# Null-key attention folded into differences, and the key transposes moved to another PSUM bank

## The chip, the cores and the metric

The kernel runs on one core of a Trainium2 chip. The metric is device time in microseconds (us) from one launch. Three runs of the kernel before gave 1120.65, 1121.5 and 1123.69 us; the median is 1121.5 us. For this kernel a difference under about 0.3% (3.4 us) cannot be told from no change.

The core has five engines with queues of their own. In the profile PE is the matrix engine (PEld its weight loads), DVE the vector engine, ACT the scalar engine, POOL the general-purpose engine and SP a queue that only issues transfers (DMAs). An engine works through its queue in order; a semaphore holds an instruction back until another engine or a transfer has done its part. SBUF is the core's working memory of 128 partitions; PSUM holds what PE writes, in banks.

## What is computed

`x` holds 64 sequences of 128 tokens with 512 channels. Attention has 16 heads of 64, and all heads share one set of keys and values. One more key and value, the null key and null value (`cond_64[0]` and `cond_64[1]`), stand in front of the 128 of each sequence, with a bias of their own per head, and the causal mask and the key mask spare them.

```
xn   = layernorm(x) * g_in
q    = (xn @ Wq) as 16 heads of 64, scaled by 1/8
k, v = xn @ Wkv                          # 64 columns each, shared by the heads
k    = [null_kv[0]; k]    v = [null_kv[1]; v]
sim  = q k^T + [null_bias | attn_bias]   # 129 columns
sim  = -max where key > token, or where the key is masked
out  = softmax(sim) v  ->  @ Wo  ->  layernorm * g_out
y    = x + out
```

A softmax is unchanged when the same number is taken from a whole row. Values can have a constant taken off and put back behind the softmax, since its weights sum to one.

## The kernel before

Sequences are blocks, numbered 0 to 63, and four make a group. One loop, `step(n)` for n from -6 to 62, interleaves the stages of different blocks by hand: in step n the values of block n are multiplied by the softmax, the scores of block n+2 are made, block n+1 goes through the exponentials, the keys and values of block n+6 are projected, and the queries of group (n+6)//4 are made. The order of the calls in `step` is the order of each engine's queue; nothing is reordered later. `part` is (n+6) mod 4, so it runs 0, 1, 2, 3, and even steps have part 0 or 2.

**PE.** Queries are made two blocks against two blocks with seven products in place of eight (`product`, line 422, banks "a", "c" and a "w"), the output projection likewise for pairs of blocks (`out_product`, line 750, banks "X", "Y" and a "w"). Pairs are blocks (1,2), (3,4) and so on up to (57,58). For a pair, products 1 and 2 and two `out_part` belong to the even step n = p+1, products 5, 6, 7 and 3 to the odd step n = p+2, and the layer norm and the residual to the even step n = p+3. So an odd step opens bank "Y" with product 5 (`pyY`), and an even step puts normalised outputs there (`yn`, line 804), one block after the other.

**The null key before.** The dot product of the queries with the null key is a linear function of the tokens, so 16 columns of weights (`wq` times the null key, summed per head, lines 862 to 880) are appended to the 128 columns of `wkv`. `kv_mm` (line 308) multiplies a block's tokens by these 144 columns, eight passes of PE per block. `kv_out` copies the keys (twice, side by side) to SBUF (line 320), and adds `vnb` to the 64 values and the 16 null scores (line 324). `nulls_move` brings values and null scores to the other half of the partitions with two copies on ACT (lines 332, 333) and two transfers on SP (lines 334, 337), in steps of part 3 and part 0. `null_copy` (line 475) puts the null scores into the first and the last column of the score tile `S`, which has 1+64+128+1 columns per head pair; `bias_add` (line 466) has filled the 192 between with bias plus mask.

**Bank "w" and the keys.** `ps_w` has two banks that are handed round. In each step `values` takes two for the attention output `po` (line 636), ACT empties them at the end of `values_end` (line 680), and the tile `pk` for the transposed keys (line 342) and for the key and value projection (line 308) takes the next. `pk` is made behind the query product 6, and read by DVE at the end of the step (lines 347, 320, 324).

**DVE in an even step.** From the instruction `done` (line 668), which waits for PE's first half of the attention output, the queue goes: residual of the second block of a pair (`pair_residual`, lines 808 and 809: `yn` times `gob` in place in bank "Y", then plus `res` into SBUF), the 32x32 transposes of the softmax (575), row maxima (513), the second scores (508), queries (443), row maxima (513), `kT` (347), `ktok` (320), `vs` (324).

**POOL in an even step** scales the softmax (line 543). In steps of part 0 it makes the four token differences `xS` for the next group as well (`token_sum`, line 404): one behind the first scale, and two behind the second. `out_sums` (730 to 733) follows.

**SP** issues the transfers; 14 of them move each block's transposed softmax (`aTb`, line 601).

Of the kernel before, what the change touches and what calls it, by code (L numbers as in the profile page):

```python
# [17 lines left out]
def kernel(  # L18
# [70 lines left out]
    KVN = 2 * DH + H  # L89
# [60 lines left out]
    nkb = const.tile([P, DH], FP, name="nkb")  # L150
    nvb = const.tile([P, DH], FP, name="nvb")
    nv2 = const.tile([P, 1], FP, name="nv2")
    nbh = const.tile([P, H], FP, name="nbh")
    biasp = const.tile([P, R8, NL + N], FP, name="biasp")
# [13 lines left out]
    for kc in (3, 1):  # L168
        nc.sync.dma_start(out=wq[:, kc, :], in_=wq_r[:, kc, :])
    nc.sync.dma_start(out=nkb, in_=cond[0].partition_broadcast(P))  # L170
    nc.sync.dma_start(
        out=wkv[:, :, 0 : 2 * DH], in_=w_kv.rearrange("(kc p) f -> p kc f", p=P)
    )

    def load_second():
        for m in (4, 5, 6):
            load_x(m)
        load_bias(1)
        load_mask(0)
        nc.sync.dma_start(out=nbh, in_=null_bias.partition_broadcast(P))  # L180
        nc.sync.dma_start(out=nvb, in_=cond[1].partition_broadcast(P))
        for r in range(2):
            nc.sync.dma_start(
                out=nv2[r * DH : (r + 1) * DH, :], in_=cond[1].unsqueeze(1)
            )

    def load_bias(u):
        rows = slice(u * DH, (u + 1) * DH)
        bias_r = attn_bias.rearrange("(u f r) i j -> u r i f j", u=2, r=2)[u]
        for r in range(2):  # L190
            rf = slice(r * NF, (r + 1) * NF)
            nc.sync.dma_start(out=biasp[rows, rf, 0:NL], in_=bias_r[r, 0:DH, :, 0:NL])
            nc.sync.dma_start(out=biasp[rows, rf, NL:], in_=bias_r[r, DH:N])

    def causal(u):

        rows = slice(0, P if u else DH)
        for keys, base in ((slice(0, NL), -DH * u), (slice(NL, NL + N), DH - DH * u)):
# [9 lines left out]

    def load_late():
# [7 lines left out]
    nc.gpsimd.memset(biasp[0:DH], 0.0)  # L217

# [7 lines left out]
    vnb = const.tile([P, DH + H], FP, name="vnb")  # L226
# [7 lines left out]
    xT, qT, kT, vs, nv, mneg = {}, {}, {}, {}, {}, {}  # L234
# [66 lines left out]
    ktok = {}  # L301

# [13 lines left out]

    def kv_out(m, pkv):
        g, t = divmod(m, GB)
        k = bp.tile([P, 2, DH], FP, tag="ktok", name=f"ktok_{m}")
        nc.vector.tensor_copy(k, pkv[:, 0:DH].unsqueeze(1).broadcast_to([P, 2, DH]))  # L320
        ktok[m] = k
        if t == 0:
            vs[g] = hp.tile([P, GB, DH + H], FP, tag="vs", name=f"vs_{g}", bufs=3)
        nc.vector.tensor_tensor(vs[g][:, t, :], pkv[:, DH:], vnb, ALU.add)

    def nulls_move(g, ts):

        if ts.start == 0:
            nv[g] = hp.tile([P, GB, DH + H], FP, tag="nv", name=f"nv_{g}")
        lo, hi = slice(0, DH), slice(DH, P)  # L330
        n1, n0 = slice(DH, DH + R8), slice(DH + R8, DH + H)
        nc.scalar.copy(nv[g][lo, ts, n1], vs[g][lo, ts, n0])
        nc.scalar.copy(nv[g][hi, ts, n0], vs[g][hi, ts, n1])
        nc.sync.dma_start(
            out=nv[g][hi, ts, 0 : DH + R8], in_=vs[g][lo, ts, 0 : DH + R8]
        )
        nc.sync.dma_start(out=nv[g][lo, ts, n0], in_=vs[g][hi, ts, n0])
# [110 lines left out]
    def mask_neg(g):  # L448
        mneg[g] = gp.tile([P, GB, NL + N], FP, tag="mneg", name=f"mneg_{g}", bufs=1)
        m8 = m8s.pop(g).rearrange("p (t j) -> p t j", t=GB)  # L450
        for keys, m in ((slice(0, NL), m8[:, :, 0:NL]), (slice(NL, NL + N), m8)):
            nc.vector.tensor_scalar(
                mneg[g][:, :, keys], m, 0.0, NEG, ALU.is_equal, ALU.mult
# [6 lines left out]
    def bias_add(b):  # L460
# [3 lines left out]
        else:  # L464
            S[b] = sp.tile([P, R8, ROW], FP, tag="s", name=f"s_{b}")
        nc.gpsimd.tensor_tensor(  # L466
            S[b][:, :, 1 : ROW - 1],
            biasp,
            mneg[g][:, t].unsqueeze(1).broadcast_to([P, R8, NL + N]),
            ALU.add,  # L470
        )

    def null_copy(b):
        g, t = divmod(b, GB)
        nc.gpsimd.tensor_copy(
            S[b][:, :, 0 : ROW : ROW - 1],
            nv[g][:, t, DH:].rearrange("p (k e) -> p e k", k=2),
        )

# [154 lines left out]
    def value_mm(b, u, half, keys, vals, slots, start=True):  # L634
        for r in range(2):
            nc.tensor.matmul(  # L636
                pos[b][u][r * DH : (r + 1) * DH, half],
                vals[keys, b % GB, 0:DH],
# [8 lines left out]
    def values(b, split):  # L647
# [6 lines left out]
        g = b // GB  # L654
# [5 lines left out]
        value_mm(b, 0, 0, lo, vs[g], slice(0, 2))  # L660
        value_mm(b, 1, 0, hi, nv[g], slice(0, 2))
        if split:
            value_mm(b, 0, 1, lo, vs[g], slice(2, 4))
            value_mm(b, 1, 1, hi, vs[g], slice(4, 6))
# [4 lines left out]
        else:  # L669
            value_mm(b, 0, 1, slice(0, P), vs[g], slice(2, 4))  # L670
            value_mm(b, 1, 1, slice(0, P), vs[g], slice(4, 6))

    def values_end(b, split):
        g = b // GB
        if split:
            value_mm(b, 1, 1, lo, vs[g], slice(4, 6), start=False)
            value_mm(b, 0, 1, hi, vs[g], slice(2, 4), start=False)
# [128 lines left out]
    def pair_residual(b):  # L806
        z = yn.pop(b)
        nc.vector.tensor_tensor(z, z, gob, ALU.mult)
        nc.vector.tensor_tensor(ys[b], z, res.pop(b), ALU.add)
# [42 lines left out]
    prods = {}  # L852

    def null_order(out, heads):

        for u in range(2):
            nc.vector.tensor_copy(
                out[:, (1 - u) * R8 : (2 - u) * R8].rearrange("p (r f) -> p r f", r=2),
                heads[:, u * R8 : (u + 1) * R8].rearrange("p (f r) -> p r f", r=2),
            )  # L860

    def weights_kv_prod(kc):

        pool, tag = ((sp, "s"), (sp, "s"), (hp, "sb"), (hp, "xb"))[kc]
        bufs = None if kc < 2 else 1
        prods[kc] = pool.tile([P, H, DH], FP, tag=tag, name=f"prod_{kc}", bufs=bufs)
        nc.gpsimd.tensor_tensor(
            prods[kc],
            wq[:, kc, :].rearrange("p (h d) -> p h d", d=DH),
            nkb.unsqueeze(1).broadcast_to([P, H, DH]),  # L870
            ALU.mult,
        )

    def weights_kv(kc):
        nc.vector.tensor_scalar(
# [438 lines left out]
```

## Time and profile before

| what | number |
|---|---|
| runs of the kernel, device time | 1120.65, 1121.5, 1123.69 us |
| profiled execution, first to last instruction | 1117.9 us |
| median of the runs less this span | 3.6 us |
| granted PE clock | 0.9 or more of full speed in all 40 slices |
| DMA engines | 116 GB/s mean, 2 to 6 tenths busy |
| `kv_mm` | 488 passes in the loop, 24 in the fill, 144 columns each |
| `null_copy` on POOL | 64 x 205 ns |

For the profiled execution its span is given and no other time; the three runs lie 2.8 to 5.8 us above that span. The page of the profile gives for each engine the busy time, its share of the span and the instructions; then the engines by slices of the span; the chain of work that ended last; and groups of instructions with their mean duration and the engine's idle time in front of them. Other views of the same trace give groups by shape, single stretches of time instruction by instruction, and the waits by who waited for whom. A row of a stretch reads: start in us, duration in us, engine, line, operation, output<-inputs, shape, count, and in brackets the idle time before it with what ended it.

### The profile page before, as it was taken

The page shows a single profiled execution, that of the slowest core. Times are in us where ns is not written, and L with a number is a line of the kernel's source. Part 1 is how long each engine was busy: PE and PEld are TensorE (multiplying, and loading weights), DVE is VectorE, ACT ScalarE, POOL GpSimd, SP SyncE. Part 2 cuts the span into 40 slices and gives each one's busy share as a digit, 9 for nine tenths or more (in the row PEclk, how much of TensorE's full clock was granted, in tenths as well). Part 3 has the DMA queues.
Part 4 walks back from the last instruction along what each step waited for, and adds up shares of the span by engine and source line. Part 5 has one row for each costly group of instructions (what it writes and reads, how often), then busy time and mean ns, then how long its engine had stood idle before and what let it go on. Part 6 is the DMA issues. An engine that isn't in the chain of part 4 may idle for free.

```text
span 1117.9 us, 27535 instructions
## 1 busy us (share of the span) xinstructions
PE 1088.6 (97%) x9794; PEld 875.1 (78%) x9794; DVE 808.8 (72%) x1743; ACT 676.5 (61%) x2709; POOL 743.0 (66%) x587
## 2 busy tenths in 40 slices
PE   8899999999999999999999999999999999999987
PEld 6576788888888788888888888888888888888633
DVE  6576578777768767777877877877776786666862
ACT  2365577565667566667656667756666765657651
POOL 6446967577676667758566676757767675677832
PEclk9999999999999999999999999999999999999999
DMA  5323244443634534354343534444353453422333
GB/s 189 125 70 71 79 137 125 128 118 91 169 97 126 132 108 131 101 149 113 128 127 89 159 100 138 124 128 119 93 168 99 125 133 114 106 68 76 98 106 99
DMA packets 107864, 130.09 MB, mean 116 GB/s; under 512 B 29264, under 2 KB 72528, under 8 KB 105936
## 3 DMA queue, kind: packets, MB, share of 16 engines
q1 hardware_dynamic: 106480, 126.96, 40.1%
q8 instruction: 78, 1.28, 0.5%
q10 hardware_dynamic: 1248, 1.38, 0.4%
q14 instruction: 58, 0.48, 0.1%
HBM read 54.86 MB, written 31.46 MB: 77 GB/s over the span
## 4 chain that ended last, share of the span: by engine, by line
PE 70%; DVE 7%; DMA 7%; SPq 6%; POOL 4%; issue 3%; ACT 3%; POOLq 0%; DVEq 0%; ACTq 0%
PE pa L422 15%; PE pyX L750 14%; PE pyY L750 7%; PE ps L495 7%; PE po L636 7%; PE pc L422 7%; DMA x<-in_x_dram 6%; SPq L601 4%; PE pk L308 4%; PE pw L422 3%; PE pyw L750 3%; PE py L697 2%; ACT s L522 2%; POOL s L466 1%; SPq L295 1%
## 5 line engine op out<-in xcount | busy, mean ns | idle before, releaser
L522 ACT ACTIVATE s<-s,nmax 128x65 f32<-128x65 f32 (+1 forms) x1024 | 372.0, 368 | 0.4
L466 POOL TENSOR_TENSOR s<-biasp,mneg 128x1536 f32<-128x1536 f32 x64 | 221.1, 3455 | 101.4 <-DVE sb L575 98.2
L543 POOL TENSOR_TENSOR s<-s,rinv 128x512 f32<-128x512 f32 (+1 forms) x128 | 189.3, 1479 | 122.8 <-DVE nmro L794 89.8
L680 ACT ACTIVATE oT<-po,nv 128x512 f32<-128x512 f32 x128 | 80.9, 683 | 200.1 <-PE po L636 198.8
L522 ACT ACTIVATION_READ_ACCUMULATOR s<-s,nmax 128x1 f32 x1024 | 194.7, 190 | 0.0
L750 PE MATMUL pyX<-wT,oT 128*128 128x256 f32 x696 | 164.8, 380 | 0.5 <-DVE kyu L762 0.5
L750 PEld LDWEIGHTS pyX<-wT,oT 128*128 128x128 f32 x696 | 131.8, 190 | 19.7 <-DVE kyu L762 0.9
L495 PEld LDWEIGHTS ps<-kT,qT 64*64 64x64 f32 x4096 | 94.2, 133 | 45.4 <-DVE s L508 23.1
L508 DVE TENSOR_TENSOR s<-ps,s 128x512 f32<-128x512 f32 (+1 forms) x128 | 121.5, 949 | 8.1 <-PE ps L495 6.6
L422 PE MATMUL pa<-xS,wq 128*128 128x256 f32 x480 | 123.5, 380 | 1.0 <-ACT ku L433 1.0
L495 PE MATMUL ps<-kT,qT 64*64 64x64 f32 (+1 forms) x4096 | 118.0, 249 | 3.6 <-DVE s L508 2.7
L513 DVE TENSOR_REDUCE nmax<-s 128x8 f32<-128x520 f32 (+1 forms) x128 | 120.1, 939 | 1.5
L575 DVE STREAM_TRANSPOSE sb<-s 128x1536 f32<-128x1536 f32 x62 | 110.0, 1774 | 13.4 <-POOL s L543 6.5
L636 PE MATMUL po<-aTb,vs 64*64 64x256 f32 (+1 forms) x1240 | 119.1, 378 | 0.0
L433 ACT COPY ku<-pa 128x256 f32<-128x256 f32 x120 | 44.6, 372 | 88.4 <-PE pa L422 88.2
L422 PEld LDWEIGHTS pa<-xS,wq 128*128 128x128 f32 x480 | 86.7, 190 | 11.2 <-ACT ku L433 1.8
L308 PE MATMUL pk<-wkv,xT 128*128 128x144 f32 x488 | 69.9, 286 | 0.0
L422 PE MATMUL pa<-xS,wS 128*128 128x256 f32 x240 | 67.8, 405 | 0.0
L443 DVE TENSOR_TENSOR qT<-pw,kp 128x256 f32<-128x256 f32 x60 | 25.4, 424 | 56.9 <-ACT kp L433 56.9
L636 PEld LDWEIGHTS po<-aTb,vs 64*64 64x64 f32 (+1 forms) x1240 | 57.4, 133 | 10.2 <-issue 3.8
L308 PEld LDWEIGHTS pk<-wkv,xT 128*128 128x128 f32 x488 | 63.4, 191 | 0.1
L804 ACT ACTIVATE yn<-y,nmro,rstdo 128x512 f32<-128x512 f32 x58 | 45.3, 782 | 29.2 <-DVE nmro L794 29.2
(120 smaller groups left out, 2096.3 us busy)
## 6 DMA issues: line engine op xcount, KB each, us to landing
aTb<-sb SPq DMA_DIRECT2D x369, 64.0 KB
x<-in_x_dram SPq DMA_DIRECT2D x64, 256.0 KB
res<-in_x_dram SPq DMA_DIRECT2D x64, 256.0 KB
out_dram<-y SPq DMA_DIRECT2D x64, 256.0 KB
aTb<-sb SPq DMA_DIRECT2D x492, 32.0 KB
xd<-xb SPq DMA_DIRECT2D x14, 1024.0 KB
xT<-xd SPq DMA_DIRECT2D x56, 256.0 KB
wo<-in_L_cond_Wo_dram SPq DMA_DIRECT2D x1, 2048.0 KB
```

The lines of the kernel that those rows point to most:

```text
L308: nc.tensor.matmul(pkv, xT[g][:, t, kc, :], wkv[:, kc, :], start=(kc == 0), stop=(kc == KC - 1),)
L422: nc.tensor.matmul(prod[tag], w[:, kc, f * P : (f + 1) * P], t[:, :, kc, :], start=(start and kc == 0), stop=(kc == HK - 1), skip_group_ch ...
L466: nc.gpsimd.tensor_tensor(S[b][:, :, 1 : ROW - 1], biasp, mneg[g][:, t].unsqueeze(1).broadcast_to([P, R8, NL + N]), ALU.add,)
L495: nc.tensor.matmul(pv[u * DH : (u + 1) * DH, r, f, :], qT[g][rows, f, t, hf, u], kT[b][rows, 0:nk], start=True, stop=True,)
L508: nc.vector.tensor_tensor(sv, pss.pop((b, hf)), sv, ALU.add)
L513: nc.vector.tensor_reduce(nmax[b][:, hf], S[b][:, :, WITH_NULL[hf]], AX.X, ALU.max, negate=True)
L522: nc.scalar.activation(row, row, AF.Exp, bias=nmax[b][:, hf, k : k + 1], accum_out=rsum[b][:, hf, k : k + 1],)
L543: nc.gpsimd.tensor_tensor(sv, sv, rinvs.pop((b, hf)).unsqueeze(2).broadcast_to([P, R8, sv.shape[2]]), ALU.mult,)
L575: nc.vector.transpose(sb.rearrange("p j e q -> p e j q"), S[b][:, :, 1 : ROW - 1].rearrange("p e (j k) -> p e j k", k=Q),)
L636: nc.tensor.matmul(pos[b][u][r * DH : (r + 1) * DH, half], vals[keys, b % GB, 0:DH], aT_of(b)[keys, slots, r * NF : (r + 1) * NF], start=s ...
L680: nc.scalar.activation(oT[b][:, u * NF : (u + 1) * NF, :].rearrange("p f (s q) -> p s f q", q=Q), po[u].rearrange("p h i f q -> p (h i) f q"),
L750: nc.tensor.matmul(prod[key], h[:, c, :], w[:, c, :], start=(start and c == 0), stop=(c == HC - 1), skip_group_check=not start,)
```

## The change

There is no column for the null key any more. The null key is taken from every key and the null bias from every bias, so the null column's score is zero in every row; the null value is taken from every value, as before.

- `wkv` keeps 128 columns (`KVN = 2*DH`). The weight products and sums for the null columns are gone (`weights_kv_prod`, `null_order`), and one instruction on DVE scales `wkv`.
- `kv_out` subtracts the null key and the null value while it reads `pk`: the copy of the keys becomes a subtraction, the addition to 80 columns a subtraction in 64.
- `biasp` and `mneg` get the two outer columns, zero; `mneg` is one constant tile. `bias_add` covers all 1552 columns, and `null_copy` is gone.
- `null_shift` subtracts the null bias from the biases at the start, once per half of the partitions, on DVE, behind each `causal`.
- `nulls_move` becomes `values_move`: one transfer in place of two, and no copy on ACT.
- In steps from 0 on, `pk` is taken from bank "Y", and the keys are transposed straight behind `values_end`, ahead of the query product 6; `kv_mm` stays where it was and fills the same tile. In earlier steps it stays in a bank "w".
- `pair_residual` multiplies `yn` from bank "Y" into the SBUF tile `ys`, and adds `res` there, in place.

```diff
-    KVN = 2 * DH + H
+    KVN = 2 * DH
...
-    nkb = const.tile([P, DH], FP, name="nkb")
-    nvb = const.tile([P, DH], FP, name="nvb")
+    nkv = const.tile([P, KVN], FP, name="nkv")
+    nbp = const.tile([P, R8], FP, name="nbp")
...
-    biasp = const.tile([P, R8, NL + N], FP, name="biasp")
+    biasp = const.tile([P, R8, ROW], FP, name="biasp")
...
-    nc.sync.dma_start(out=nkb, in_=cond[0].partition_broadcast(P))
...
-        nc.sync.dma_start(out=nvb, in_=cond[1].partition_broadcast(P))
+        nc.sync.dma_start(
+            out=nkv, in_=cond[0:2].rearrange("r d -> (r d)").partition_broadcast(P)
+        )
...
+    def null_shift(u):
+        rows = slice(u * DH, (u + 1) * DH)
+        nc.vector.tensor_copy(
+            nbp[rows].rearrange("p (r f) -> p r f", r=2),
+            nbh[rows, u * R8 : (u + 1) * R8].rearrange("p (f r) -> p r f", r=2),
+        )
+        nc.vector.tensor_tensor(
+            biasp[rows, :, 1 : ROW - 1],
+            biasp[rows, :, 1 : ROW - 1],
+            nbp[rows].unsqueeze(2).broadcast_to([DH, R8, NL + N]),
+            ALU.subtract,
+        )
...
-        nc.vector.tensor_copy(k, pkv[:, 0:DH].unsqueeze(1).broadcast_to([P, 2, DH]))
+        nc.vector.tensor_tensor(
+            k,
+            pkv[:, 0:DH].unsqueeze(1).broadcast_to([P, 2, DH]),
+            nkv[:, 0:DH].unsqueeze(1).broadcast_to([P, 2, DH]),
+            ALU.subtract,
+        )
...
-        nc.vector.tensor_tensor(vs[g][:, t, :], pkv[:, DH:], vnb, ALU.add)
+        nc.vector.tensor_tensor(vs[g][:, t, :], pkv[:, DH:], nkv[:, DH:], ALU.subtract)
...
-        nc.scalar.copy(nv[g][lo, ts, n1], vs[g][lo, ts, n0])
-        nc.scalar.copy(nv[g][hi, ts, n0], vs[g][hi, ts, n1])
-        nc.sync.dma_start(
-            out=nv[g][hi, ts, 0 : DH + R8], in_=vs[g][lo, ts, 0 : DH + R8]
-        )
-        nc.sync.dma_start(out=nv[g][lo, ts, n0], in_=vs[g][hi, ts, n0])
+        nc.sync.dma_start(out=nv[g][hi, ts], in_=vs[g][lo, ts])
...
         nc.gpsimd.tensor_tensor(
-            S[b][:, :, 1 : ROW - 1],
+            S[b],
             biasp,
-            mneg[g][:, t].unsqueeze(1).broadcast_to([P, R8, NL + N]),
+            mneg[:, t].unsqueeze(1).broadcast_to([P, R8, ROW]),
             ALU.add,
         )
-
-    def null_copy(b):
...
     def pair_residual(b):
         z = yn.pop(b)
-        nc.vector.tensor_tensor(z, z, gob, ALU.mult)
-        nc.vector.tensor_tensor(ys[b], z, res.pop(b), ALU.add)
+        nc.vector.tensor_tensor(ys[b], z, gob, ALU.mult)
+        nc.vector.tensor_tensor(ys[b], ys[b], res.pop(b), ALU.add)
...
+    def weights_kv():
+        nc.vector.tensor_tensor(
+            wkv, wkv, gin.unsqueeze(2).broadcast_to([P, KC, KVN]), ALU.mult
+        )
...
+        pks = []
+        if ok(mkv) and mkv >= GB - 1:
+            pks.append(None)
+
+        def keys_T(pool, tag):
+            pks[0] = pool.tile([P, KVN + N], FP, tag=tag, name=f"pk_{mkv}")
+            k_T(mk, pks[0][:, KVN:])
...
             values_end(n, split)
             if n > B3 + 1:
                 out_mm(n - 1, NF)
+        if pks and ok(n):
+            keys_T(ps_y, "Y")
...
-        if ok(mkv) and mkv >= GB - 1:
-
-            pk = ps_w.tile([P, KVN + N], FP, tag="w", name=f"pk_{mkv}")
-            k_T(mk, pk[:, KVN:])
-            kv_mm(mkv, pk[:, 0:KVN])
+        if pks:
+            if not ok(n):
+                keys_T(ps_w, "w")
+            kv_mm(mkv, pks[0][:, 0:KVN])
...
         if n == -6:
-            for kc in range(1, KC):
-                weights_kv_prod(kc)
             causal(1)
+            null_shift(1)
             load_bias(0)
-            for kc in range(2):
-                weights_kv(kc)
+            weights_kv()
         if n == -5:
-            for kc in range(2, KC):
-                weights_kv(kc)
             causal(0)
+            null_shift(0)
             mask_neg(0)
-            nc.vector.tensor_scalar(vnb[:, 0:DH], nvb, -1.0, None, ALU.mult)
-            null_order(vnb[:, DH:], nbh)
```

## The prediction

> **What bounds the kernel now.** I read the page first: its head, busy times and chain.
>
> ```profile
> span 1117.9 us, 27535 instructions
> ...
> PE 1088.6 (97%) x9794; PEld 875.1 (78%) x9794; DVE 808.8 (72%) x1743; ACT 676.5 (61%) x2709; POOL 743.0 (66%) x587
> ...
> PE 70%; DVE 7%; DMA 7%; SPq 6%; POOL 4%; issue 3%; ACT 3%; POOLq 0%; DVEq 0%; ACTq 0%
> ```
>
> PE is the bound: only 29 us of the span lack a matmul, so work taken from DVE, ACT or POOL is worth nothing by itself, and a new wait of PE costs in full. Then I read one even step and the start of the next odd one, instruction by instruction (columns: start, duration, engine, line, operation).
>
> ```profile
> 515.81 1.91 POOL L543 TENSOR_TENSOR s<-s,rinv 128x1024 f32<-128x1024 f32 x1 [1.35 <-DVE nmro L794]
> 516.96 0.16 DVE L668 COPY done<-po 128x1 f32<-128x1 f32 x1 [0.43 <-PE po L636]
> 517.68 1.28 POOL L404 TENSOR_TENSOR xS<-xT 128x512 f32<-128x512 f32 x1
> 517.76 0.69 DVE L809 TENSOR_TENSOR y<-yn,res 128x512 f32<-128x512 f32 x1
> 518.37 1.77 DVE L575 STREAM_TRANSPOSE sb<-s 128x1536 f32<-128x1536 f32 x1
> 519.12 0.27 PE L342 MATMUL pk<-ident,ktok 128*128 128x128 f32 x1
> 519.23 1.15 PE L308 MATMUL pk<-wkv,xT 128*128 128x144 f32 x8
> 520.22 1.03 PE L422 MATMUL pa<-xS,wq 128*128 128x256 f32 x4
> 523.46 1.70 PEld L750 LDWEIGHTS pyY<-wT,yS 128*128 128x128 f32 x8
> 523.62 0.23 DVE L324 TENSOR_TENSOR vs<-pk,vnb 128x80 f32<-128x80 f32 x1
> 523.67 1.89 PE L750 MATMUL pyY<-wT,yS 128*128 128x256 f32 x8
> ```
>
> Two things are to be seen. DVE runs from `done` at 516.96 without a gap, in ten more instructions, to the end of `vs` at 523.85, the last reader of `pk`. And PE loads the weights of product 5 for bank "Y" at 523.46 and streams from 523.67: 0.39 and 0.18 us before `vs` ends. I compared these two at all 29 products 5: 26 (158 to 986 us) have this picture, the load between 0.37 and 0.40 us before the end of `vs`, and `vs` 6.89 us behind the start of `done`. Last, a place in the fill where DVE and POOL meet.
>
> ```profile
> 53.99 1.27 POOL L404 TENSOR_TENSOR xS<-xT 128x512 f32<-128x512 f32 x1 [4.71 <-ACT xT L269]
> 54.92 1.42 DVE L390 TENSOR_TENSOR wq<-wq 128x1024 f32<-128x1024 f32 x1
> 55.34 2.13 POOL L404 TENSOR_TENSOR xS<-xT,xS 128x512 f32<-128x512 f32 x1
> ```
>
> L390 has both inputs in SBUF. It starts while POOL works, and ends 1.08 us after POOL's instruction has ended (55.26); 1024 elements at its rate elsewhere are that long. POOL's next takes 2.13 in place of 1.27, and ends 1.13 behind L390. The two took turns.
>
> **The change, part by part.**
>
> *Narrower key and value projection.* Eight passes of 144 columns take 504.36 less 503.37 in the odd step, 0.99 us, or 124 ns each. A pass of 128 columns, the transpose in front, takes 0.11 (519.12 to 519.23). So a block saves 8 x 14 ns = 0.11 us. Of 64 blocks three fall into the fill and 26 into even steps ahead of a product 5, where (below) the wait swallows them: 35 x 0.11 = 3.9 us saved. The ends are 0 and 64 x 0.11 = 7.0.
>
> *Transpose straight behind the values.* PE's order and count are the same. The first pass after 64x64 tiles pays for its weight load: 0.10 us where product 6 is first, 0.06 where a transpose was (69.97 to 70.14, against 0.11 in the row above). About 0.05 us in 28 odd steps: 1.4 saved; ends 0 and 58 x 0.05 = 2.9. The tile needs bank "Y", free when DVE has read `yn` (L808, over at 517.72 in the worst, the even step); PE comes at 518.1. No wait there, unless L808 is 0.4 us late. One stall at 84.15 (0.54 us, PE on the emptying of `po` by ACT) goes; the next thing late is the copy `ku` behind it, so 0.3 is left.
>
> *Bank "Y" held to the end of the even step.* This is the new wait. Before, product 5 waited for the other inputs and for `yn`, long read; now it waits for `vs`, which ends behind it, and everything on PE stands behind product 5. From the end of a DVE instruction to PE's load is 0.05 us (L508 ends at 500.78, PE's load at 500.83), and a load that nothing covers costs another 0.10 before the columns stream. `vs` with 64 columns in place of 80 ends 0.02 earlier. So streaming moves from 0.18 before to 0.14 after the old end of `vs`: 0.32 us, 26 times, 8.3 us. What PE saves earlier in the even step only lengthens the wait, since the DVE chain starts at `done`. Ends: 0 if `vs` were over in time, 0.42 x 26 = 10.9 if the load's whole delay counts. The subtraction of the null key costs DVE nothing against the copy: 128 columns at the slope of L324 (231 ns for 80) make 0.28, the copy's row.
>
> *Residual through SBUF.* L808 writes SBUF, as L508 does from PSUM (687 ns for the same 512 columns, against 695). L809 had one input in PSUM and now has both in SBUF, like L390. Where POOL works, it waits. In the 13 even steps of part 0 (n = 6, 10, ... 54) POOL runs L404 behind L543 without a pause, and L809 starts while it runs. From L809's start to the end of that POOL instruction I find, in the 13 places, 0.45 to 1.29 us, mean 1.02 (1.20 in the rows above). From this go 0.14, the part of a DVE instruction that needs no data (L390 lost only 0.19 of 0.34), and 0.28, because two ACT copies of 0.19 and 0.20 leave these steps, the exponentials end earlier and with them L543 and L404; not 0.4, since `kp` then waits for PE. That leaves 0.60 x 13 = 7.8 us. All of it comes out at product 5, because DVE has no slack between L809 and `vs`; products 3 and 5 on PE are late next. Ends: 0 if the port is free or DVE gets in first, 13 x 1.15 = 15 if all are like the longest. In the steps of part 2 L543 ends within 0.06 of L809's start and POOL is then idle: nothing. The first residual of a part-0 step meets an L404 too (513.18 against 513.24); DVE waits for ACT and PE there for about 1 us anyway, so nothing, with 0.45 x 13 = 5.9 as the upper end where PE's `po` would wait for the bank.
>
> [...]
>
> [...] Rows of this trace differ: 1024 columns take 1211 ns from PSUM (L508) and 1216 to 1224 from SBUF (L385 to L387). I keep the rows and take no gain.
>
> *Fill.* PE stalls 3.86 us at 41.44 on ACT's `xT`, and behind that lies DVE's chain: weight scalings, reductions and reorderings of 13 us, half of it waiting for POOL. What replaces it: two subtractions of 1536 elements (1.73 each by L508's slope), each behind POOL's `causal`, and one scaling. The second `causal` needs transfers that were issued from 24.67 behind the first; they can now go from about 21.8, when the load of x ahead of them is out. DVE reaches the statistics of token block 6 at about 30.1 in place of 32.0: 1.9 us, and 0.3 on three projections, 2.2 saved. Ends 0 and 4.
>
> *Nothing:* `null_copy` (64 x 0.2 us) and its waits leave POOL, which is not on the path; `bias_add` grows by 1% (0.04); one transfer and two ACT copies per move go. In part-0 steps PE stalls up to 1.5 us on `aTb` transfers, and one issue less (0.63) shortens that, but there product 5 now waits for a chain that POOL starts, so no gain.
>
> *Drain.* L809 at 1043.16 meets an L466 of 3.45 us that began at 1041.44, and the second scores stand behind it: up to 1.7 lost; product 5 at 1049.25 no longer waits for L809 (0.36). I take +1.0; ends -1 and +3.
>
> **Sum.** -3.9 - 1.4 - 0.3 + 8.3 + 7.8 - 2.2 + 1.0 = +9.3 us on a span of 1117.9, and on the median of the runs, 1121.5: 1130.8, so 1131.
>
> **Rivals.** *The wait without the lock:* L809 reads two SBUF tiles undisturbed. For it: the lock on two inputs has one instance here. Then 7.8 goes, and about 3 us of `aTb` stalls with it: -1.5, 1120. *No wait at "Y", faster:* `vs` ends at least 0.32 us earlier against product 5, so that bank "Y" is free in time; that decides it. L809 would have to shrink from 0.69 to 0.37, since nothing else on the chain changes. For it: both its operands leave PSUM. Against: the rows of 1024 columns above. Then the 8.3 goes too, and the even steps keep their 26 x 0.16: -14, 1107.5. *POOL keeps the port through three instructions in a row* (L404, L404, L730), 2.5 us more in 13 steps: +42, 1163. Against it stands the fill, where POOL ran three products from 17.05 and DVE's L875 got in after the first.
>
> **How the numbers follow.** Forecast 0.66, with its own range 1124 to 1140 from the ends of the lock and the wait; no lock 0.18 (1117 to 1123); no wait 0.10; port kept 0.03; something else 0.03. The range 1119 to 1140 leaves out the no-wait case, the kept port and the edges of the first two. A change of 0.3%, 3.4 us, is about what runs of this kernel can tell from none. Faster: no wait 0.10 and 0.05 of no lock, 0.15. Same: 0.09 of no lock and 0.05 of the forecast, 0.14. Slower: 0.71.
>
> **What would show it.** The 128-column passes 0.11 us apart; product 5's load 0.05 us behind `vs` in 26 odd steps, idle about 0.4 us for DVE; L809 of 0.69 us in part 2 and about 1.3 to 1.9 in part 0, ending with POOL's L404; the stall at 41 us down to 2. I am wrong if product 5 streams ahead of `vs`, or if L809 keeps 0.69 everywhere.

## The result, and the profile after

| | before | changed |
|---|---|---|
| runs, device time | 1121.5 us median of 5 (1120.22 to 1123.69) | 1128.77 us median of 5 (1125.68 to 1131.24) |
| span of the profiled execution | 1117.9 us | 1126.9 us (its device time 1128.77) |

The ratio of the runs is 1.0066, 95% interval 1.0043 to 1.0088. The change made the kernel 7.3 us slower; 1131 was predicted, 1119 to 1140.

The head, the busy times of the first engines and the chain of the changed kernel's page:

```profile
span 1126.9 us, 27325 instructions
...
PE 1092.5 (97%) x9794; PEld 870.2 (77%) x9794; DVE 808.7 (72%) x1729; ACT 665.7 (59%) x2645; POOL 712.6 (63%) x521
...
PE 44%; DVE 22%; DMA 14%; SPq 10%; ACT 4%; issue 4%; POOL 1%; DVEq 0%; ACTq 0%; POOLq 0%
```

ACT has 11 and POOL 30 us less to do and DVE the same as before; the time is longer all the same. The last line shows where to look: PE's share of the chain that ends last fell from 70% to 44%, and DVE's rose from 7% to 22% (DMA's from 7% to 14%, that of SP's queue from 6% to 10%). PE, still the engine with the most work, waits more for others, and for DVE above all.

The span is cut at the first matmul of product 5, which comes once per pair of blocks; a pair here is the time from one to the next. The prediction's terms are put to the places where they fall: 13 x (0.32 - 0.11 - 0.05) for the pairs with a part-2 step, the same and 7.8 for those with a part-0 step, the rest of the 9.3 at the ends.

| stretch | before | changed | difference | predicted |
|---|---|---|---|---|
| up to the first product 5 | 125.24 | 120.98 | -4.3 | with the drain: -2.7 |
| 13 pairs with a part-2 step | 426.62 | 429.09 | +2.5 | +2.1 |
| 13 pairs with a part-0 step | 434.04 | 441.70 | +7.7 | +9.9 |
| from the 27th product 5 to the end | 131.98 | 135.11 | +3.1 | (above) |

The first and the last stretch differ in one thing more, the clock granted to PE. It is 0.5 of full speed in the kernel before from 41.6 to 45.0 us, where twice eight passes of `kv_mm` take 2.19 and 1.58 us (1.15 elsewhere); the traced run of the changed kernel has no such time ahead of its first product 5. It has some in the drain, from 1051.9 to 1058.7 and from 1079.2 to 1082.6, where the kernel before has none (the last few us of both left out): there two lots of scores and a product 5 take 1.13, 1.99 and 2.80 us against 0.69, 1.10 and 1.97. So some of the -4.3 and of the +3.1 is the clock's, by these rows up to 1.5 and 2.2 us. The 26 pairs have the full clock in both kernels.

Here is a part-0 step of the changed kernel, from the first residual of the pair to product 5 (stretch of time; start, duration, engine, line, operation, and in brackets the idle time ahead of it with what ended it). The lines have moved with the diff: the residual is L813 and L814, `kp` L447, `vs` L344, product 5 L755.

```profile
511.20 1.27 POOL L418 TENSOR_TENSOR xS<-xT,xS 128x512 f32<-128x512 f32 x1
511.25 1.77 DVE L814 TENSOR_TENSOR y<-y,res 128x512 f32<-128x512 f32 x1
...
512.94 0.41 DVE L778 TENSOR_TENSOR y<-pyw,kyp 128x256 f32<-128x256 f32 x1
...
513.40 0.65 PE L641 MATMUL po<-aTb,vs 64*64 64x256 f32 x4
513.44 0.37 ACT L447 COPY kp<-pa 128x256 f32<-128x256 f32 x1 [1.09 <-DVE y L778]
...
513.84 0.42 DVE L457 TENSOR_TENSOR qT<-pw,kp 128x256 f32<-128x256 f32 x1 [0.49 <-ACT kp L447]
...
514.37 0.43 PE L641 MATMUL po<-aTb,nv 64*64 64x256 f32 x2 [0.32 <-issue]
...
514.90 1.90 POOL L548 TENSOR_TENSOR s<-s,rinv 128x1024 f32<-128x1024 f32 x1 [2.43 <-DVE nmro L799]
...
515.53 0.15 DVE L673 COPY done<-po 128x1 f32<-128x1 f32 x1
...
516.47 0.88 DVE L814 TENSOR_TENSOR y<-y,res 128x512 f32<-128x512 f32 x1
...
516.76 1.74 POOL L418 TENSOR_TENSOR xS<-xT 128x512 f32<-128x512 f32 x1
...
522.53 0.20 DVE L344 TENSOR_TENSOR vs<-pk,nkv 128x64 f32<-128x64 f32 x1
...
522.85 1.59 PEld L755 LDWEIGHTS pyY<-wT,yS 128*128 128x128 f32 x8 [0.57 <-POOL oT L736]
522.88 1.97 PE L755 MATMUL pyY<-wT,yS 128*128 128x256 f32 x8 [0.20 <-DVE vs L344]
```

From the bottom up. Product 5 now waits for `vs`: its weights are loaded 0.12 us and its columns stream 0.15 us behind the end of `vs`, in all 26 steady odd steps. That is the wait that was predicted. The second residual (516.47) takes 0.88 us where 0.69 was the rule: it starts 0.33 us before the end of POOL's L548, ends 0.55 us behind that end, and goes in ahead of POOL's L418, which is drawn out to 1.74. It takes 0.83 to 0.88 in 12 of the 13 part-0 steps and 1.79 in the last. The first residual (511.25) takes 1.77 us beside another L418 that began 0.05 us ahead of it, and that is so in all 13 part-0 steps. In the kernel before the same pair of instructions stood 0.06 us apart, and neither was slowed:

```profile
513.18 1.28 POOL L404 TENSOR_TENSOR xS<-xT,xS 128x512 f32<-128x512 f32 x1
513.24 0.69 DVE L809 TENSOR_TENSOR y<-yn,res 128x512 f32<-128x512 f32 x1
...
513.85 0.41 DVE L773 TENSOR_TENSOR y<-pyw,kyp 128x256 f32<-128x256 f32 x1
...
514.35 0.37 ACT L433 COPY kp<-pa 128x256 f32<-128x256 f32 x1
...
514.76 0.42 DVE L443 TENSOR_TENSOR qT<-pw,kp 128x256 f32<-128x256 f32 x1 [0.49 <-ACT kp L433]
```

What follows the slow addition is late: `y` (L778), then PE's `po`, and with a detour over ACT's `kp` the second bank of `po`: the profile names no releaser for it, but it starts 0.11 us behind the end of `qT` (L457, 514.26), which reads that bank out. The wait of `kp` for `y` stands 13 times in the changed kernel's list of waits (us in total, times, longest), and not in that of the kernel before:

```profile
ACT kp L447 <- DVE y L778: 14.3, 13, 1.1
```

The groups by shape of the changed kernel (behind the bars: busy us and mean ns of one, idle us ahead of them with what ended it):

```profile
L479 POOL TENSOR_TENSOR s<-biasp,mneg 128x1552 f32<-128x1552 f32 x64 | 205.8, 3216 | 118.6 <-DVE sb L580 115.4 <-DVE mneg L465 2.7 <-PE paL L620 0.4
...
L321 PE MATMUL pk<-wkv,xT 128*128 128x128 f32 x488 | 64.3, 275 | 0.0
...
L814 DVE TENSOR_TENSOR y<-y,res 128x512 f32<-128x512 f32 x58 | 59.3, 1023 | 2.0
L755 PE MATMUL pyY<-wT,yS 128*128 128x256 f32 x232 | 57.8, 393 | 6.6 <-DVE vs L344 6.5
```

58 additions at 1023 ns, where the kernel before had 692: 19 us more on DVE.

### The profile page after: what moved, and what is told of

The parts are those of the page before. It is cut to its first block, busy times and chain, and to the rows that moved or that the text cites. A ratio compares the mean times of both kernels' runs of the same rounds, so it can differ in the third digit from the quotient of the medians.

```text
span 1126.9 us, 27325 instructions
## 1 busy us (share of the span) xinstructions
PE 1092.5 (97%) x9794; PEld 870.2 (77%) x9794; DVE 808.7 (72%) x1729; ACT 665.7 (59%) x2645; POOL 712.6 (63%) x521
## 4 chain that ended last, share of the span: by engine, by line
PE 44%; DVE 22%; DMA 14%; SPq 10%; ACT 4%; issue 4%; POOL 1%; DVEq 0%; ACTq 0%; POOLq 0%
PE pyX L755 9%; SPq L606 8%; PE pa L436 7%; DMA x<-in_x_dram 7%; PE pyY L755 6%; DVE sb L580 4%; DVE nmax L518 4%; PE ps L500 4%; PE po L641 4%; PE pc L436 3%; DVE s L513 3%; PE py L702 3%; ACT s L527 3%; PE pk L321 2%; PE pq L387 2%
## 5 line engine op out<-in xcount | busy, mean ns | idle before, releaser
L479 POOL TENSOR_TENSOR s<-biasp,mneg 128x1552 f32<-128x1552 f32 x64 | 205.8, 3216 | 118.6 <-DVE sb L580 115.4
L548 POOL TENSOR_TENSOR s<-s,rinv 128x512 f32<-128x512 f32 (+1 forms) x128 | 189.5, 1481 | 134.4 <-DVE nmro L799 101.0
L755 PE MATMUL pyX<-wT,oT 128*128 128x256 f32 x696 | 164.6, 379 | 0.5 <-DVE kyu L767 0.5
L755 PEld LDWEIGHTS pyX<-wT,oT 128*128 128x128 f32 x696 | 132.0, 190 | 19.3 <-DVE kyu L767 0.9
L513 DVE TENSOR_TENSOR s<-ps,s 128x512 f32<-128x512 f32 (+1 forms) x128 | 121.4, 949 | 10.7 <-PE ps L500 10.3
L447 ACT COPY ku<-pa 128x256 f32<-128x256 f32 x120 | 44.7, 373 | 79.7 <-PE pa L436 79.7
L261 POOL TENSOR_TENSOR rstd<-rstd,nhalf 128x1 f32<-128x1 f32 x64 | 35.6, 558 | 56.5 <-DVE rstd L260 54.4
L457 DVE TENSOR_TENSOR qT<-pw,kp 128x256 f32<-128x256 f32 x60 | 25.4, 424 | 64.0 <-ACT kp L447 64.0
L321 PE MATMUL pk<-wkv,xT 128*128 128x128 f32 x488 | 64.3, 275 | 0.0
```

The costliest lines, as they stand in the source:

```text
L321: nc.tensor.matmul(pkv, xT[g][:, t, kc, :], wkv[:, kc, :], start=(kc == 0), stop=(kc == KC - 1),)
L479: nc.gpsimd.tensor_tensor(S[b], biasp, mneg[:, t].unsqueeze(1).broadcast_to([P, R8, ROW]), ALU.add,)
L513: nc.vector.tensor_tensor(sv, pss.pop((b, hf)), sv, ALU.add)
L548: nc.gpsimd.tensor_tensor(sv, sv, rinvs.pop((b, hf)).unsqueeze(2).broadcast_to([P, R8, sv.shape[2]]), ALU.mult,)
L755: nc.tensor.matmul(prod[key], h[:, c, :], w[:, c, :], start=(start and c == 0), stop=(c == HC - 1), skip_group_check=not start,)
```

## The experiments

Theory A is the prediction's: the time is a wait at bank "Y" and the exclusion of an addition of two SBUF tiles by POOL, against what the narrower projection and the fill save. Theory B, formed on the trace above, keeps both causes but moves the second: its cost is at the *first* residual, and it reaches PE through the banks "w". The kernel before was run beside every group of kernels: 1121.1 to 1121.9 us.

**The parts taken singly.** Three kernels, each the changed kernel with one or both of its other two parts undone: the first hunk of this diff alone is `keys_in_Y`, the other two alone are `sbuf_residual`, all three are `nulls_alone`.

```diff
-        nc.vector.tensor_tensor(ys[b], z, gob, ALU.mult)
-        nc.vector.tensor_tensor(ys[b], ys[b], res.pop(b), ALU.add)
+        nc.vector.tensor_tensor(z, z, gob, ALU.mult)
+        nc.vector.tensor_tensor(ys[b], z, res.pop(b), ALU.add)
...
-        if pks and ok(n):
-            keys_T(ps_y, "Y")
...
-            if not ok(n):
-                keys_T(ps_w, "w")
+            keys_T(ps_w, "w")
```

> The changed kernel with both of its other parts undone: the keys are transposed where they were, in a bank "w", and the residual multiplies in bank "Y" as before. What is left is that there are no null columns. Theory of the wait and the lock: these two cost everything, and the narrower projection pays in all steps: 64 x 0.11 = 7.0 us, the fill 4.3 as measured in the change, the aTb stalls of part 0 about 1.5 less: 1108.7 us (1106 to 1112), product 5's weights loaded 0.35 us or more ahead of the end of vs. Rival, the DVE chain from done paces the pairs even without bank Y: only the fill and the odd steps gain, 1113 to 1117. Rival, the null columns' removal is itself what costs (bias_add over 1552 columns, the subtractions): 1121 or more.

> The changed kernel with only the residual put back (yn times gob in place in bank "Y", then plus res into SBUF). The wait at bank "Y" stays, the two SBUF inputs go. Theory of the wait and the lock: the residual's addition is 0.69 us in all steps again; the 13 pairs of part 0 lose what they have over those of part 2, 13 x 0.4 = 5, the drain about 2: 1122 us (1118 to 1124), and product 5 is still loaded 0.12 us behind vs in 26 places. That the bank is released only by the addition makes PE wait some 0.35 us ahead of the transpose, which the wait at product 5 swallows. Rival, the slow additions are a symptom and something else delays part 0: 1127 to 1130.

> The changed kernel with only the keys put back into a bank "w" at their old place; the residual goes through SBUF. Theory of the wait and the lock: the first addition of a part-0 step still takes 1.7 us beside POOL, and the row sums, po and the second scores come late behind it: 0.5 to 0.7 us in each of 13 steps, 2 in the drain, on top of the kernel without null columns alone (expected 1108.7): 1117 us (1114 to 1121). Rival, without the wait at product 5 the late additions are hidden: within 2 us of that kernel, 1109 to 1111.

| kernel | median us (runs) | ratio to before, 95% | 13 part-2 pairs | 13 part-0 pairs |
|---|---|---|---|---|
| nulls_alone | 1108.8 (1107.64 to 1109.39) | 0.9871 to 0.9902 | 423.98 | 429.49 |
| keys_in_Y | 1117.28 (1115.89 to 1118.77) | 0.9945 to 0.9976 | 430.97 | 431.73 |
| sbuf_residual | 1123.62 (1121.31 to 1130.83) | 1.0011 to 1.0042 | 423.80 | 444.34 |
| changed | 1128.77 (1125.68 to 1131.24) | 1.0043 to 1.0088 | 429.09 | 441.70 |

Leaving out the null columns alone makes the kernel 12.5 us faster, as expected to a tenth. The keys in bank "Y" cost 8.5 us on top of that, the SBUF residual 14.8, both together 20.0: each hides a part of the other. The wait falls on both kinds of pair: against `nulls_alone`, `keys_in_Y` has 7.0 us more in part-2 pairs and 2.2 in part-0 pairs. The SBUF residual falls on part-0 pairs, where POOL works beside it, and leaves part-2 pairs as they were (423.80 against 423.98). One of the part-0 pairs of `sbuf_residual`, 36.34 us long, holds 3.4 us at half the granted clock; its neighbours take 34.1 and 34.4, so some 2 of the 444.34 us are not the residual's. The residual's cost was taken too low in both expectations: 11.5 us with the keys in bank "Y" where 7 was expected, 14.8 with them in "w" where 8 was.

In the kernel with only the keys in bank "Y", the same stretch has a second wait: the transpose (L356) now waits for the addition that releases the bank.

```profile
514.17 0.69 DVE L814 TENSOR_TENSOR y<-yn,res 128x512 f32<-128x512 f32 x1
...
514.91 0.14 PEld L356 LDWEIGHTS pk<-ident,ktok 128*128 128x128 f32 x1 [0.50 <-DVE y L814]
...
520.19 0.21 DVE L344 TENSOR_TENSOR vs<-pk,nkv 128x64 f32<-128x64 f32 x1
...
520.52 1.59 PEld L755 LDWEIGHTS pyY<-wT,yS 128*128 128x128 f32 x8 [0.46 <-issue]
520.55 1.75 PE L755 MATMUL pyY<-wT,yS 128*128 128x256 f32 x7
```

In this place the transpose streams 0.11 us later behind `po` than in the changed kernel, in the other 25 places 0.31 to 0.35 us later (some 0.35 was expected), and product 5 still waits for `vs`. So the SBUF residual has a gain of its own: with it bank "Y" comes free earlier, and the part-2 pairs are 1.9 us shorter in all (429.09 against 430.97).

**The wait at bank "Y", taken away by order alone.** On DVE, `kT`, `ktok` and `vs` are moved in even steps ahead of the row maxima of the second scores.

```diff
+        if pks and first:
+            pk = pks.pop()
+            kT_out(mk, pk[:, KVN:])
+            kv_out(mkv, pk[:, 0:KVN])
+        if fast:
             if late and sc:
                 scores_max(nb, 1)
```

> The changed kernel with one thing moved on DVE: in even steps kT, ktok and vs are read out of bank "Y" ahead of the row maxima of the second scores instead of behind them. Nothing else. Theory of the wait: vs ends by the maxima's 1.1 us earlier against done, so product 5 no longer waits for it; the 0.36 to 0.44 us stalls go, 26 x 0.4 = 10.4, and the lock stays: 1118.5 us (1115 to 1121). Rival, the maxima come 0.5 us later instead, the exponentials of the odd step with them, and the same wait turns up at the scores or at po: 1126 to 1130.

Measured: 1122.45 us, with runs from 1117.61 to 1128.71. In the stretch of this kernel, `vs` ends 0.70 us ahead of product 5's load:

```profile
518.38 0.20 DVE L344 TENSOR_TENSOR vs<-pk,nkv 128x64 f32<-128x64 f32 x1
...
518.51 1.20 DVE L518 TENSOR_REDUCE nmax<-s 128x8 f32<-128x1032 f32 x1
...
519.28 1.70 PEld L755 LDWEIGHTS pyY<-wT,yS 128*128 128x128 f32 x8
...
519.50 1.89 PE L755 MATMUL pyY<-wT,yS 128*128 128x256 f32 x8
```

The part-2 pairs fell from 33.0 to 32.5 us each (422.67 together), as short as in any kernel here: the wait was no more than DVE's order, and nothing took its place there. The part-0 pairs stayed at 441.21 us: the wait at product 5 is gone, but in five of them PE now waits 0.39 to 1.22 us for `y` (L778) ahead of `po`, behind the slow addition. The traced run, 1119.6 us, is 1.1 above the expected 1118.5. The median is 4 above it and outside the expected range; the runs of this kernel spread over 11 us, to which the last section comes back.

**Which of the two residuals.** Only the first, or only the second of a pair, is put back into bank "Y"; for the second the condition is `not paired(b)`.

```diff
-        nc.vector.tensor_tensor(ys[b], z, gob, ALU.mult)
-        nc.vector.tensor_tensor(ys[b], ys[b], res.pop(b), ALU.add)
+        o = z if paired(b) else ys[b]
+        nc.vector.tensor_tensor(o, z, gob, ALU.mult)
+        nc.vector.tensor_tensor(ys[b], o, res.pop(b), ALU.add)
```

> The changed kernel with only the first residual of a pair put back (in place in bank "Y"); the second, behind done, still goes through SBUF, and the keys stay in bank "Y". Theory that the lock costs at the first residual (it holds up the emptying of both banks "w", and po with it): the 13 pairs of part 0 fall from 34.0 to about 33.4 us, since the second addition of 0.88 adds 0.2 to the wait at product 5: 1119 us (1117 to 1121). Rival, the prediction's own account (first residual nothing, second 0.60 each): no change, 1128 to 1130.

> The mirror image: only the second residual of a pair put back in bank "Y", the first through SBUF. Theory that the lock costs at the first residual: little is won, since done comes late all the same, and PE now waits at the transpose for the bank: 1125 to 1129 us. Rival, the prediction's own account: 1128.8 less 7.8, 1121 us (1119 to 1123).

Measured: 1118.19 us (1117.27 to 1123.12) with the first put back, 1127.95 (1125.66 to 1129.85) with the second. So the first residual carries 10.6 of the 11.5 us. Putting back the second gains 0.8, which the runs cannot tell from nothing: its 13 part-0 pairs gain 1.4 (440.35 against 441.70), but PE's transpose waits for the bank again, by which the part-2 pairs lose 2.1 (431.24 against 429.09). That wait is 0.32 to 0.35 us in part-2 pairs, but only 0.09 in 12 of the 13 part-0 pairs, 1.4 us in all of these. So the slow second addition is worth 1.4 to 2.8 us there. Theory A had the two the other way round.

**How the slow addition reaches PE.** ACT's copies `kp` (query product 1) and `kyp` (output product 1) share one SBUF slot, so `kp` waits until DVE has read `kyp` in `y` (L778), right behind the slow addition. In this kernel (keys in bank "w", residual through SBUF) the slot is split. The same line splits a second slot, which the copy of output product 5 shares with the query copy `u3`; in the waits of neither kernel does one of these two copies wait for a reader of the other, and the part-2 pairs, which have such copies too, gained nothing (424.21 against 423.80).

```diff
-        kept[name] = bp.tile([P, HE], FP, tag=f"k{slot}", name=f"k{name}", bufs=1)
+        kept[name] = bp.tile([P, HE], FP, tag=f"o{slot}", name=f"k{name}", bufs=1)
```

> The kernel with the residual through SBUF and the keys in bank "w" (1123.6 us), with one thing more: ACT's copy kp gets an SBUF slot of its own instead of the one that it shares with kyp, so that it need not wait for DVE's y (L778), which stands behind the slow addition. Theory that the late addition reaches PE on two legs, y (L778) before the first bank of po, and y, kp, qT (L457) before the second: the second leg shortens by the idle 0.49 us that DVE spends on kp, po with nv no longer waits 0.47: 13 x 0.45 = 5.9 less, 1117.7 us (1116 to 1120). Rival, the second stall of po has another cause (transfers of aTb): within 1.5 us of 1123.6.

The stretch behind the first residual of a part-0 step, in the kernel with the residual through SBUF and the slot shared:

```profile
577.38 1.77 DVE L814 TENSOR_TENSOR y<-y,res 128x512 f32<-128x512 f32 x1
...
579.07 0.41 DVE L778 TENSOR_TENSOR y<-pyw,kyp 128x256 f32<-128x256 f32 x1
...
579.53 0.65 PE L641 MATMUL po<-aTb,vs 64*64 64x256 f32 x4 [0.36 <-DVE y L778]
579.57 0.37 ACT L447 COPY kp<-pa 128x256 f32<-128x256 f32 x1 [1.10 <-DVE y L778]
...
579.97 0.42 DVE L457 TENSOR_TENSOR qT<-pw,kp 128x256 f32<-128x256 f32 x1 [0.49 <-ACT kp L447]
...
581.67 0.15 DVE L673 COPY done<-po 128x1 f32<-128x1 f32 x1
```

And the same stretch of the kernel with the slot split:

```profile
572.40 1.77 DVE L814 TENSOR_TENSOR y<-y,res 128x512 f32<-128x512 f32 x1
...
573.50 0.37 ACT L447 COPY kp<-pa 128x256 f32<-128x256 f32 x1
...
574.09 0.41 DVE L778 TENSOR_TENSOR y<-pyw,kyp 128x256 f32<-128x256 f32 x1
...
574.42 0.41 DVE L457 TENSOR_TENSOR qT<-pw,kp 128x256 f32<-128x256 f32 x1
...
576.05 0.16 DVE L673 COPY done<-po 128x1 f32<-128x1 f32 x1 [0.31 <-PE po L641]
```

The addition takes 1.77 us in both. In the first, `kp` starts behind `y`, DVE idles 0.49 us for it, and `done` is 4.29 us behind the addition's start. In the second, `kp` runs beside the slow addition, and `done` comes after 3.65. The time fell to 1113.37 us (1110.94 to 1115.82), 10.2 less and not the 5.9 expected. By the trace the exponentials behind `kp` on ACT come earlier too, and with them DVE's `rinv` and what is queued behind it (the scores, L513, begin 2.66 us behind the addition's start and not 3.69), which the expectation left out. So of the 14.8 us some 10 reach PE only through the shared buffer slot; with the slot split the slow additions cost 4.6 (1113.37 against 1108.8).

The same line in the changed kernel, everything else as it was:

> The changed kernel with one thing more: kp in an SBUF slot of its own. The slow additions stay (1.77 us at the first residual of part 0), the wait at product 5 stays. Theory that the slow addition reaches PE mostly through ACT's copy kp, which waits for DVE's y (L778) because they share a slot: part 0 loses most of its lateness as in the kernel with the keys in bank "w" (10 us there), less what the wait at product 5 keeps, 2 to 3: 1121 us (1118 to 1123). Rival, with the keys in bank "Y" the wait at product 5 decides part 0 whatever the copy does: 1127 to 1130.

Measured: 1118.79 us (1116.49 to 1120.91), ratio 0.9959 to 0.9981: 10.0 us less than the changed kernel and 0.2 to 0.4% faster than before. No `kp` waits for `y` any more. Its additions still average 1013 ns, `vs` still holds product 5 up in 26 places, and the part-0 pairs are 432.40 us together, 0.7 above those of the kernel without the SBUF residual.

**Versions without either cost.** First: first residual in bank "Y", `vs` ahead of the maxima (the two diffs above together). Second: that, the split slot, and the second residual in bank "Y" in part-0 steps too (`o = z if paired(b) or b % GB == 0 else ys[b]`). Third: the kernel that only leaves out the null columns, with `vs` ahead and the split slot.

> The changed kernel with the first residual in bank "Y" as before, and kT, ktok and vs ahead of the row maxima in even steps. Keys stay in bank "Y", the second residual goes through SBUF. Theory: the wait at product 5 is gone as it was with the values first (part-2 pairs 32.50), the lock is left with 0.19 in 13 steps, which now has slack in front of it: part-0 pairs near 33.0; 1107 us (1105 to 1110), level with the kernel that only leaves out the null columns (1108.8). Rival, the second addition still decides part 0: 1112 to 1116.

> The changed kernel with kT, ktok and vs ahead of the row maxima in even steps, kp in an SBUF slot of its own, the first residual of a pair in bank "Y" and the second too where POOL is busy beside it (steps of part 0); only the second residual of part 2 goes through SBUF. No addition of two SBUF inputs meets POOL any more. Theory: part-2 pairs stay at 32.50; part-0 pairs lose the second lock (0.19 to 1.1, eleven of them) and gain the transpose's wait for the bank, 0.42, half of which slack takes: 1106.5 us (1104 to 1109). Rival, the transpose's wait passes on in full: 1109 to 1112.

> The kernel that only leaves out the null columns (1108.8 us), with kT, ktok and vs ahead of the row maxima in even steps, and kp in an SBUF slot of its own. Theory: product 5 did not wait for vs there, and kp not for y, so neither has anything to give: 1108.8 within 1.5 us. Rival, DVE's order in the even steps still holds PE up (the 0.1 us by which part-2 pairs were shorter with the values first, 32.50 against 32.60): 1106 us.

Measured: 1108.1 (1106.97 to 1109.22), 1107.84 (1106.14 to 1108.95) and 1107.26 us (1106.47 to 1109.81), against 1108.8 for the null columns alone. All are 1.1 to 1.2% faster than before, and runs cannot tell them apart. So the keys in bank "Y" have no gain to show even where product 5 does not wait for them: the part-2 pairs of the first two are 422.79 and 423.02 us against 424.13 of the third, their part-0 pairs 431.62 and 431.29 against 429.41.

## Why the prediction was right, and where it was not

*Narrower projection:* right. With it alone the part-2 pairs are 2.64 us shorter, 0.20 each; two blocks times 0.11 were predicted. That the wait would swallow the share of the even steps holds too: against `nulls_alone`, the part-2 pairs of the changed kernel are longer by 0.39 us each (429.09 against 423.98), and 0.32 + 0.11 - 0.05 = 0.38 follows from the prediction.

*Transpose straight behind the values:* right. Against their pitch, the first two passes of product 6 behind the values lost 0.09 and 0.10 us each step; now the transpose loses 0.09 and product 6 behind it 0.06. That is the 0.05 that was predicted. The stall at 84.15 went and one on `ku` came, as said, but of the same size (PE idle for 0.51 us at 81.16, against 0.54): nothing gained there, not 0.3.

*Bank "Y" held:* right in place and count, and in size where it can be told apart. The columns of product 5 stream 0.147 us behind `vs` in 26 steps; 0.15 was predicted, as 0.05 to the weight load and 0.10 from there, and it came as 0.12 and 0.03. The part-2 pairs grew by 2.5 us (2.1 predicted). That the part alone cost 8.5 us beside 8.3 is no confirmation: its 7.0 us in part-2 pairs hold the transpose's wait too, and in part-0 pairs it cost only 2.2. The rival *no wait at "Y"* is excluded; its deciding point, `vs` earlier against product 5, was reached only by moving it on DVE, and there the wait did go.

*Residual through SBUF:* the wait for POOL is there, in the size predicted per instruction: an addition ends 0.53 to 0.55 us behind the POOL instruction that was there first, the 0.69 less the 0.14 that the prediction took from L390's row (that this part of an instruction needs no data was the author's reading, and is not shown). The step that failed is that of the first residual, "DVE waits for ACT and PE there for about 1 us anyway, so nothing". The waits of DVE lie *behind* `y`, and one of them is for `kp`, which itself waits for `y`. Nothing stood idle between the residual and `y` (L773) in 12 of the 13 places of the kernel before; that row was there to be read. The cost came where the upper end had put it, at `po` and its bank, but it is 10.6 us and not 5.9 at most, since the addition lost 1.08 us and not 0.45. The second residual, priced at 0.60 each or 7.8, cost 0.8 to 2.8: the slow first one holds up the row sums and POOL's L548 as well, so in 12 of 13 steps the second addition meets the end of L548, and enters ahead of L418, 0.14 to 0.19 us longer than alone. With the first residual in its bank, the second is slowed in 7 of the 13 steps, by 0.11 to 1.12 us.

*The sum of the pairs.* The runs with parts undone take the sum apart (us in 13 pairs; null columns: `nulls_alone` against before; keys: `keys_in_Y` against that; residual: the changed kernel against that). The prediction's terms are 26 x 0.11, 13 x 0.38 (as above) and 13 x 0.60.

| part | part-2 pairs, predicted | measured | part-0 pairs, predicted | measured |
|---|---|---|---|---|
| no null columns | -2.9 | -2.6 | -2.9 | -4.6 |
| keys in bank "Y" | +4.9 | +7.0 | +4.9 | +2.2 |
| residual through SBUF | 0 | -1.9 | +7.8 | +10.0 |
| together | +2.1 | +2.5 | +9.9 | +7.7 |

In part-2 pairs 1.9 us of the keys' cost is the transpose's wait for the addition, which the SBUF residual takes away again. In part-0 pairs the residual cost more than its price, for another reason than the one given, and the other two parts less; that the total came out near is luck. Undone in another order the parts would have other shares, since each hides some of the other. Why the keys cost so little in part-0 pairs was not settled.

Before the runs, that such an addition waits for POOL had one row behind it, L390's. The 13 first additions, each ending 0.54 to 0.55 us behind the end of POOL's L418, bear it out, so the rival *the wait without the lock* (1120 us) is wrong as to the lock. No run shows the 7.8 of the sum, which took that row for 13 second residuals: these cost 0.8 to 2.8 us, the first ones 10.6. Nor does any run show a port: what is seen is that DVE and POOL take turns. That POOL goes on through three instructions, as the rival of 1163 us has it, is wrong: DVE got in between two POOL instructions (L814 of 0.88 us, L418 drawn out to 1.74). Nor does it pay that an operand leaves PSUM: undisturbed additions are 0.69 us with two SBUF inputs, and 0.69 with one in PSUM.

*Fill:* the sign is right. PE's stall of 3.86 us at 41.44 is now 1.50 at 38.60 and 0.31 at 40.04, near the 2 expected. The -4.3 us up to the first product 5 lie just past the end given (4), but they hold two odd steps and the narrower passes there too, and up to 1.5 us of them are the granted clock's, for which the prediction has no term. *Drain:* +3.1 against +1.0, just past the end given. The addition that was priced takes 1.72 us beside POOL's L479 (1048.68); the next one, left out, takes 1.52 (1055.30); and 10.2 us at half the granted clock fall into the same stretch. In `sbuf_residual` and `values_first`, with both additions slow but 3.4 us at half clock in place of the 10.2, the stretch is +1.3 and +0.7. So a good part of the 3.1 seems to go with the clock. Why the clock fell there was not settled.

In all, the ends brought -1.1 us where -2.7 was predicted, the pairs +10.1 where +12.0 was, and the medians of the runs differ by 1.7 us less than the traced executions: 1131 came within 2.3 us because errors of both signs cancelled, which is luck.

## What to carry to other kernels

Before a slowed instruction is costed at nothing because its engine waits a little later anyway, ask what that wait is for: if its releaser hangs on the slowed instruction, by data or by a shared buffer slot, there is no slack. Where a change bundles parts, build them apart: here one part was worth 12.5 us and the other two cost 20. Bank "Y", given a second user, came free late by its new last reader's place in DVE's queue (product 5 streamed 0.15 us behind `vs` in 26 steps), and moving that reader alone took 6.3 us off (1128.77 to 1122.45): look at the reader's place before moving the bank.

## What the runs showed that was not expected

- `bias_add` on POOL takes 3216 ns for 1552 columns in whole rows, and took 3455 ns for 1536 columns between two left out; in three kernels without null columns it is 3206 to 3216. Whether the missing gaps or the first column's place do it was not separated. POOL has 4% of the chain that ends last before and 1% after.
- Two copies of 0.37 us that share one SBUF slot decided 10 us. Without the slow addition a slot of its own gains nothing that the runs can tell (1107.26, with another edit, against 1108.8).
- In the profiled run with the residual through SBUF and the keys in "w", part-0 pairs vary from 33.4 to 36.3 us; the longest holds 3.4 us, from 513.7, in which the clock granted to PE is 0.5 of full speed. Runs of the kernels with the slow first addition in reach 1130.8 and 1128.7 us where their medians are 1123.62 and 1122.45. These two runs have the lowest mean granted clock of their kernels, 0.990, where the others have 0.991 to 0.997. So the clock goes with the spread; 0.005 of 1122 us is some 6 us if PE paces all of it, an estimate from these figures. What lowers it, and whether PE's waits behind the slow addition do, was not settled. The 40 slices of the page hardly show such stretches: they are 28 us wide, and only one of the changed kernel's falls to 8 tenths.
